# The last stage of a four-layer image kernel, rebuilt on pairs of positions

## The chip, the cores and the metric

The kernel runs on one core of one Trainium2 chip. A time is the device time of one execution in microseconds (us) on that core.

In profile lines PE is TensorE, PEld its weight loads, DVE is VectorE, ACT is ScalarE, POOL is GpSimd, and SPq is the queue of SyncE that issues transfers. "L1168" is a line of the source.

## The reference

Four images of 192 channels and 64x64 points in float32 pass through four layers. The change concerns the third and fourth only. Cut to these:

```python
# layer 3: a depthwise conv whose weights come from the pooled image; of the 3x3 taps only four are kept
pooled = x.mean(axis=(2, 3))
t = relu(gamma * (pooled @ w1.T - running_mean) * rsqrt(running_var + EPS) + beta)
wt = (t @ w2.T + b2).reshape(b * DIM, 1, 3, 3) * MASK        # MASK keeps taps 0, 1, 2 and 3
x = conv(x, wt, groups=b * DIM, padding=1) + bias

# layer 4: sedenion product in windows of 4x4, then an MLP
xn = layer_norm(x, norm1_g, norm1_b)                          # over the 192 channels
xw = get_window(xn)                                           # 16 positions of 192 channels each
xw = xw @ sedenion_full_weight(w_sed)                         # y[k] = sum over s of +-(xw[s] @ w_sed[s ^ k])
y = gelu(reverse_window(xw)) @ proj_w + proj_b
x = x + y
h = gelu(layer_norm(x, norm2_g, norm2_b) @ fc1_w + fc1_b)     # 768 hidden channels
x = x + h @ fc2_w + fc2_b
```

The first two layers are three Mamba blocks. They take the first three quarters of the time and are left as they are.

## The kernel before

192 channels are kept as two chunks of 96 (`CP = 96`). A position of the 4x4 window is a set of 256 columns (`NWIN = 256`, one per window), and `T = 512` columns are two positions. The parts that matter, with cuts marked:

```python
def conv(img):
    ...                                        # pooled sums, squeeze-excite, weights wt of this image
    for s in range(NPOS):                      # 16 positions, 2 chunks, 4 taps: all on DVE
        for k in range(2):
            for tap in (3, 0, 1, 2):
                ...
                nc.vector.scalar_tensor_tensor(o, src, wk, o, ALU.mult, ALU.add)
    return xw

def product(xn, q, background):                # positions 2q and 2q+1
    for h in range(2):
        k = 2 * q + h
        ...
        for m in range(2):                     # output chunk of 96
            for sign, ps in ((1, plus), (-1, minus)):
                of = [s for s in range(NPOS) if signs[s][k] == sign]
                for n, s in enumerate(of):
                    for cc in range(2):        # input chunk of 96
                        nc.tensor.matmul(ps[:, m, :], w["sed"][:, cc, s ^ k, bass.ts(m, CP)],
                                         xn[:, cc, bass.ts(s, NWIN)], ...)
                    if n % 2:
                        background.step()      # post() of the pair before: project, norm, MLP
        nc.scalar.copy(neg, minus)
        nc.vector.tensor_tensor(y[:, :, bass.ts(h, NWIN)], plus, neg, ALU.subtract)

class Norm:                                    # variance as 128x4 numbers, spread again by a matmul
    ...
    nc.tensor.matmul(var[:, q : q + 1], sq[:, k, bass.ts(q, 128)], self.mean_w[:, 0:1], ...)
    nc.scalar.activation(rs, var, AF.Sqrt, bias=self.eps)
    nc.vector.reciprocal(rs, rs)
    ...
    nc.tensor.matmul(rb[:, bass.ts(q, 128)], rs[:, q : q + 1].to_broadcast([128, CP]), self.ident, ...)

for b in range(NB):                            # the serial frame: conv, first norm, product
    xw = conv(img)
    if b + 1 < NB:
        img = load(b + 1)
    for t in range(NT):
        for _ in ln.run(xw[:, :, c], ..., xn[:, :, c]):
            pass
    for q in range(NPOS // 2):
        y = product(xn, q, background)
        background.drain()
        background.add(post(b, q, xw, y, outs))
    background.drain()
```

## Time and profile before

| | before |
|---|---|
| time, median of the runs beside the changed kernel | 13043.12 us (13041.86 to 13043.54) |
| last stage in the profile | 9637 to 13042.5 us |
| opening (stage start to first product matmul) | 131 us |
| one image | 840 us |
| two positions of one image | 85.4 us |

The prediction shows the page's slices, three stretches of the last stage, and the timeline of the product. One line completes them, the opening by stretch: busy us of PE, weight loads, DVE, ACT and POOL (with the number of instructions), then granted clock, DMA share and GB/s.

```profile
9637.00:9768.00 131.00, 14.82 (x52) 10.15 (x53) 80.42 (x140) 4.26 (x7) 1.87 (x8) 0.50 0.36 66
```

In 131 us DVE works 80 and PE 15. What fills DVE are the conv taps, 649 ns each in the mean of 384, with no idle time ahead of them: the conv is bound by DVE alone, four times over.

### The profile page before, as it was taken

What the parts mean: (1) busy time and instruction counts of PE and PEld (TensorE: products, weight loads), DVE (VectorE), ACT (ScalarE), POOL (GpSimd) and SP (SyncE); (2) the same over time, 40 slices, a digit from 0 to 9 for tenths busy, and PEclk for the clock granted to TensorE, in tenths of its full rate; (3) what the DMA queues carried; (4) which work ended last, traced back from release to release, by engine and by line L of the source; (5) the groups of instructions that cost most, each with busy time, mean ns of one, the idle gap of its engine ahead of it and who ended that gap; (6) DMA issues with size and microseconds to landing.
All of it is one profiled execution on the core that took longest, in us unless ns stands there. A gap on an engine that the chain in (4) does not pass through costs nothing.

```text
span 13042.5 us, 102087 instructions
## 1 busy us (share of the span) xinstructions
PE 10585.6 (81%) x34064; PEld 4515.3 (35%) x34064; DVE 9231.5 (71%) x7740; ACT 6226.9 (48%) x8329; POOL 6565.0 (50%) x3394
## 2 busy tenths in 40 slices
PE   6777777777777777758898998989859979889799
PEld 2222222222222222222333333333326646566465
DVE  7999999999999999979887788787831030220300
ACT  5566556566556556646666656665611111111111
POOL 5777777777777777756555555555610000000000
PEclk7777777777777776767888888888869979889899
DMA  5666666666666666645444444444420000000000
GB/s 144 164 166 166 162 167 169 162 165 166 160 166 166 161 168 167 160 131 149 126 130 130 125 129 129 129 130 127 128 40 3 5 12 5 5 13 5 3 5 5
DMA packets 842950, 1449.85 MB, mean 111 GB/s; under 512 B 129194, under 2 KB 162254, under 8 KB 842326
## 3 DMA queue, kind: packets, MB, share of 16 engines
q1 hardware_dynamic: 841662, 1440.15, 42.7%
q8 instruction: 270, 4.42, 0.2%
q10 hardware_dynamic: 760, 3.16, 0.1%
q14 instruction: 258, 2.11, 0.1%
HBM read 1254.25 MB, written 188.74 MB: 111 GB/s over the span
## 4 chain that ended last, share of the span: by engine, by line
PE 44%; DVE 34%; ACT 8%; POOL 6%; issue 5%; DMA 2%; SPq 1%; DVEq 0%; ACTq 0%; POOLq 0%
DVE h L601 21%; DVE h L586 10%; PE plus L1168 7%; PE minus L1168 7%; PE ps_dw L986 5%; POOL h L614 4%; PE ps_in L483 4%; PE ps_o L331 3%; PE ps_conv L501 3%; PE ps_h L408 3%; PE ps_o L417 3%; PE y L623 2%; ACT dA L595 2%; DVE xw L1153 2%; ACT L595 1%
## 5 line engine op out<-in xcount | busy, mean ns | idle before, releaser
L601 DVE TENSOR_TENSOR_SCAN h<-dA,m_state,h 128x512 f32<-128x512 f32 x4608 | 5614.2, 1266 | 423.2 <-ACT dA L595 316.0
L614 POOL TENSOR_TENSOR h<-h,C 128x2048 f32<-128x2048 f32 x1152 | 5213.5, 4526 | 93.3 <-POOL m_state L613 1.0
L595 ACT ACTIVATE dA<-dtE,m_A 128x512 f32<-128x512 f32 x4608 | 3096.2, 687 | 2177.5 <-DVE h L601 2047.6
L586 DVE TENSOR_TENSOR h<-dtxE,B 128x2048 f32<-128x2048 f32 x1152 | 2602.9, 2259 | 109.4 <-DMA dtxE<-r_dtx 109.4
L623 PE MATMUL y<-h,gather 128*32 128x512 f32 x9216 | 1631.9, 789 | 1033.8 <-POOL h L614 1006.2
L613 POOL COPY m_state<-h 128x4 f32<-128x4 f32 x1152 | 215.2, 187 | 1922.4 <-DVE h L601 1888.9
L1179 DVE TENSOR_TENSOR y<-plus,neg 96x512 f32<-96x512 f32 x64 | 44.0, 687 | 1600.8 <-ACT neg L1178 1600.8
L483 PE MATMUL ps_in<-xT,m_in_w 96*128 96x512 f32 x1536 | 992.4, 803 | 73.9 <-ACT z L486 72.5
L1168 PE MATMUL plus<-xn,t 96*96 96x256 f32 x4352 | 1013.4, 380 | 0.0
L501 PE MATMUL ps_conv<-raw,m_conv 128*128 128x512 f32 x2112 | 951.3, 598 | 0.0
L1168 PE MATMUL minus<-xn,t 96*96 96x256 f32 x3840 | 934.3, 396 | 12.6 <-ACT xn L390 12.3
L623 PEld LDWEIGHTS y<-h,gather 128*32 128x32 f32 x9216 | 201.6, 121 | 2137.9 <-POOL h L614 1639.0
L1106 POOL MEMSET img<- 96x132 f32 x4 | 0.8, 204 | 1794.9 <-DVE xw L1153 1794.9
L1168 PEld LDWEIGHTS plus<-xn,t 96*96 96x96 f32 x4352 | 710.0, 163 | 338.0 <-issue 132.8
L1168 PEld LDWEIGHTS minus<-xn,t 96*96 96x96 f32 x3840 | 645.0, 170 | 252.1 <-ACT xn L390 29.1
L483 PEld LDWEIGHTS ps_in<-xT,m_in_w 96*128 96x128 f32 x1536 | 377.0, 260 | 782.0 <-issue 520.5
L986 PE MATMUL ps_dw<-strip,dw 96*96 96x512 f32 x1152 | 640.1, 710 | 0.0
L1178 ACT COPY neg<-minus 96x512 f32<-96x512 f32 x64 | 36.7, 573 | 1165.1 <-PE minus L1168 1165.1
L537 POOL TENSOR_TENSOR raw<-dt,xc 128x1536 f32<-128x1536 f32 x96 | 330.5, 3442 | 504.7 <-ACT dt L536 504.7
L501 PEld LDWEIGHTS ps_conv<-raw,m_conv 128*128 128x128 f32 x2112 | 387.2, 189 | 540.1 <-issue 532.8
L527 PE MATMUL ps_dt<-dbl,m_dt_w 12*128 12x512 f32 x576 | 432.0, 860 | 158.2 <-ACT dbl L519 118.1
L573 PE MATMUL B<-dbl,spread 44*128 44x512 f32 x384 | 341.6, 986 | 237.8 <-DVE h L586 237.8
(142 smaller groups left out, 11488.1 us busy)
## 6 DMA issues: line engine op xcount, KB each, us to landing
dtE<-r_dt SPq DMA_DIRECT2D x2304, 256.0 KB, 4.5
dtxE<-r_dtx SPq DMA_DIRECT2D x2304, 256.0 KB, 6.0
r_dt<-dt SPq DMA_DIRECT2D x96, 768.0 KB, 4.0
r_dtx<-raw SPq DMA_DIRECT2D x96, 768.0 KB, 7.8
x<-x SPq DMA_DIRECT2D x64, 384.0 KB, 3.1
xt<-in_x SPq DMA_DIRECT2D x32, 384.0 KB, 6.7
x<-o SPq DMA_DIRECT2D x32, 384.0 KB, 2.6
img<-x SPq DMA_DIRECT2D x8, 1536.0 KB, 20.8
```

Of the source, the lines that this page charges most:

```text
L331: nc.tensor.matmul(ps, self.w2[:, m, bass.ts(k, CP)], h[:, m, :], start=(m == 0), stop=(m == NH - 1),)
L408: nc.tensor.matmul(ps, self.w1[:, k, bass.ts(m, 128)], x[:, k, :], start=(k == 0), stop=(k == 1))
L483: nc.tensor.matmul(ps, self.in_w[:, k, bass.ts(e, 128)], xn[:, k, :], start=(k == 0), stop=(k == 1))
L501: nc.tensor.matmul(ps, self.conv[:, d, j, :], raw[:, d, j : j + T], start=(j == 0), stop=(j == K - 1))
L527: nc.tensor.matmul(ps, self.dt_w[:, bass.ts(d, 128)], dbl[:RK, :], start=True, stop=True)
L586: self.nc.vector.tensor_tensor(h, u[k // 2][1], u["B", k % 2].unsqueeze(1).broadcast_to([128, 4, T]), ALU.mult,)
L595: self.nc.scalar.activation(dA, u[k // 2][0][:, j, :], AF.Exp, scale=self.A[:, k, j : j + 1])
L601: self.nc.vector.tensor_tensor_scan(h[:, j, :], u.pop(("dA", k, j)), h[:, j, :], self.state[:, k, j : j + 1], ALU.mult, ALU.add,)
L614: nc.gpsimd.tensor_tensor(h, h, u["C", k % 2].unsqueeze(1).broadcast_to([128, 4, T]), ALU.mult)
L623: self.nc.tensor.matmul(u["ys"][32 * j : 32 * j + 32, :], self.ex.gather[:, i // 2, :], h[:, j, :], start=(i == 0), stop=(i == 3),)
L986: nc.tensor.matmul(ps, dw[:, k, j, :], s[:, k, dy : dy + rows, dx : dx + HW], start=(j == 0), stop=(j == 8),)
L1168: nc.tensor.matmul(ps[:, m, :], w["sed"][:, cc, s ^ k, bass.ts(m, CP)], xn[:, cc, bass.ts(s, NWIN)], start=(n == 0 and cc == 0), stop=(n = ...
```

## The change

It has three intents. First, fill the array: two window positions (4 apart, one row of the 4x4 window: `position(g, 0)` and `position(g, 1)`) have 384 channels together, which are three chunks of 128 instead of four of 96. The outer two chunks need all 128 columns; the middle one is half of one position and half of the other, and is made by two 64-column matmuls meant to run side by side. Second, make the next image's conv and first norm while the product of this image runs, through four lanes of generators that get one tick per product step; the normed image waits in DRAM. Third, take mean and variance both by a matrix of ones, so that they come out already spread over 128 partitions. The reciprocal then works on 128x512 instead of 128x4. Besides, one of the four conv taps goes to ACT, the norm's multiply by the reciprocal root goes from DVE to POOL, and the pooled sums come from an accumulated output in the stage before.

```diff
+PIECES = (
+    (0, slice(0, 128), slice(0, 128), 0),
+    (1, slice(0, 64), slice(128, 192), 0),
+    (1, slice(64, 128), slice(0, 64), 1),
+    (2, slice(0, 128), slice(64, 192), 1),
+)
...
+        def each(outs, wt, v, cols):          # middle chunk: 64 rows per position
+            for start in (True, False):
                 for k in range(2):
+                    c, p = (2 * k, ALL) if start else (1, half[k])
+                    nc.tensor.matmul(outs[k], wt[p, c, cols[k]], v[p, c, :], start=start, stop=not start)
+        def normed(v, which):
+            mean = bank("mean")
+            each(full(mean), ones, v, [ALL, ALL])
...
+            nc.scalar.activation(sq, d, AF.Square)
+            yield 5
+            var = bank("var")
+            each(full(var), ones, sq, [ALL, ALL])
...
+            nc.scalar.activation(rs, var[:, :, W], AF.Sqrt, bias=eps)
+            nc.vector.reciprocal(rs, rs)
+            nc.gpsimd.tensor_tensor(d[:, 0::2, :], d[:, 0::2, :], rs, ALU.mult)
...
+            yield 12
...
+        def product(b, k):
+            for m, sides in enumerate((
+                    [(0, ALL, slice(0, 128))],
+                    [(0, half[0], slice(128, 192)), (1, half[1], slice(192, 256))],
+                    [(1, ALL, slice(256, 384))])):
+                made = [terms(k, side) for side, _, _ in sides]
+                for n in range(3 * NP):
+                    for t, (_, parts, cols) in zip(made, sides):
...
+                    lanes.tick()
...
+        def mlp(b, k, x3, xn2):
...
+            nc.scalar.activation(h, h, AF.Gelu)
+            yield 5
...
+        lanes.add(2, prepare(0))
+        lanes.until(lambda: (0, NP - 1) in ready)
         for b in range(NB):
+            if b:
+                lanes.until(lambda: (b, NP - 1) in ready)
+                fetch(b)
+                lanes.until(lambda: (b - 1, NP - 1) in added and not lanes.lanes[0])
             if b + 1 < NB:
+                lanes.add(2, prepare(b + 1))
+            for k in range(NP):
+                if k > 1:
+                    lanes.until(lambda: (b, k - 2) in closed)
+                lanes.add(0, project(b, k, product(b, k)))
+        lanes.drain()
```

A `yield 5` in a lane means: go on five ticks later. One tick is one product step, that is one 256-column matmul slot (two records in the trace, 0.4315 us, as the prediction works out).

## The prediction

> **What bounds the kernel now.** I read the page first, for where the stages lie, then busy time by stretch, the groups of the last stage, and the timeline record by record.
>
> ```profile
> PE 10585.6 (81%) x34064; PEld 4515.3 (35%) x34064; DVE 9231.5 (71%) x7740; ACT 6226.9 (48%) x8329; POOL 6565.0 (50%) x3394
> ...
> PE   6777777777777777758898998989859979889799
> DVE  7999999999999999979887788787831030220300
> PEclk7777777777777776767888888888869979889899
> ```
>
> In slices 1 to 28 DVE carries the two Mamba stages, which the change leaves alone (but for one accumulated output on 64 evictions). From slice 30 on, PE is all there is. The timeline puts the last stage from 9637 us (constants and image asked for) to 13042.5: 3405 us. All of the change is there.
>
> ```profile
> 9900.00:10200.00 300.00, 300.00 (x1177) 193.03 (x1176) 26.53 (x39) 53.35 (x59) 0.00 (x0) 0.98 0.03 6
> 10475.00:10608.00 133.00, 52.52 (x138) 25.87 (x137) 77.79 (x142) 17.37 (x20) 0.75 (x3) 0.62 0.10 18
> 12986.00:13043.00 57.00, 37.72 (x86) 15.85 (x84) 7.11 (x10) 13.93 (x15) 0.00 (x0) 0.81 0.07 14
> ```
>
> Busy us of PE, weight loads, DVE, ACT and POOL, then clock, DMA share, GB/s. Within an image PE is full (300 of 300). Between images 131 to 134 us pass with PE under half busy: 28 us of the last position's remaining work, then 78 us of DVE alone (the conv). An image lasts 840 us (conv starts at 9689, 10530, 11366, 12209). The bound is PE columns in the product, and a serial conv four times.
>
> ```profile
> 10205.26 7.93 PE L1168 MATMUL plus<-xn,t 96*96 96x256 f32 x36
> ...
> 10213.03 6.21 PE L1168 MATMUL minus<-xn,t 96*96 96x256 f32 x28
> ```
>
> 36 records in 7.77 us: 0.2158 us each. An f32 matmul leaves two records (8192 in the two product groups, 4096 matmuls in the code), so 256 columns cost 0.4315 us, whatever rows and columns of the array they fill: 96x96 of 128x128 is 56%. Check: two positions take 128 x 0.4315 = 55.2 us of product plus 28.7 of projection, norm and MLP = 83.9; the trace repeats every 85.4.
>
> **What the Trainium skill says.** "TensorEngine Tiling (Array Packing)", Key Properties: tiles run in parallel, and changing the tiling mode drains the array. The trace agrees on both for column tiles:
>
> ```profile
> 976.56 4.89 PE L501 MATMUL ps_conv<-raw,m_conv 128*128 128x512 f32 x11
> 981.38 1.06 PE L623 MATMUL y<-h,gather 128*32 128x512 f32 x8
> 982.38 1.98 PE L501 MATMUL ps_conv<-raw,m_conv 128*128 128x512 f32 x4
> ```
>
> Eight gather records on four 32-column tiles take 1.06 us with drain: two slots of 0.43, not eight. From full mode to tiles the start-to-start step is 0.522 us against 0.429 inside a mode: 0.093 us a switch. No trace of before shows two row tiles at once; for those I rely on the page.
>
> "VectorE: DVE Perf Modes", First, the fixed hardware budget: Reciprocal is an iterative divide with a repeat count of 8. The trace agrees as far as it goes:
>
> ```profile
> L377 DVE RECIPROCAL ln_rs<-ln_rs x64: 177/178/179, 9763.3 to 13000.9; 128x4 f32<-128x4 f32 x64
> L1093 DVE RECIPROCAL bn_s<-bn_s x1: 155/155/155, 9661.4 to 9661.4; 48x1 f32<-48x1 f32 x1
> ```
>
> Three more elements cost 23 ns, near 8 ns each, where a tensor_tensor element costs about 1.3 (687 ns for 512). The change makes the operand 512 wide.
>
> "TensorE: Matmul & The Clock Gate", What's actually happening: a low-activity window of about 3.4 us halves the clock. The trace agrees: the burst of N=1 variance matmuls is followed by product records at half speed.
>
> ```profile
> 9977.83 1.59 PE L368 MATMUL var<-mean_w,xn 96*128 96x1 f32 x13
> 9979.28 4.02 PE L1168 MATMUL minus<-xn,t 96*96 96x256 f32 x10
> ```
>
> Ten records in 4.0 us instead of 2.3: some 1.7 us lost per burst. The same page (the architectural detail on queue depths) says ACT and DVE are strict FIFO; that decides two terms below.
>
> **The change, part by part.** I counted the built program in its order, with the tiling mode of each matmul, in slots of 0.4315 us.
>
> *PE.* A pair of positions takes 24 full matmuls, 24 pairs on two 64-column tiles, and 24 full: 72 slots instead of 128. Projection: 8 matmuls, 5 slots with pairing. Each norm: mean and variance, each 2 full plus one pair of row tiles: 6 slots. MLP: 18 + 18 slots. Sum 72+5+12+36 = 125 slots = 53.9 us per pair, against 85.4: for 32 pairs 1729 us by my count. There are 1114 changes of mode, x 0.093 = 104 us. Together 1833; 24 of it (image 0's first norm) is in the opening, so 1809.
>
> *Opening.* Image 0's conv and norm are still alone. First half image, shared with 7 MB of weights: about 40 us (39 before). Then DVE goes in strict order: 9 taps x 0.648 = 5.8; wait for mean on a cold PE 2.9; subtractions 1.55; wait for square, variance, root, beyond two taps put in between, 3.1; reciprocal 512 x 8.3 ns + 0.15 = 4.4 (an estimate from the page's count of 8 and DVE's 0.96 GHz): 17.8 us per pair. After four, the second half image must land, some 25 us, because there is one image buffer. 40 + 59 + 25 + 77 + 4 = 205 us, against 131 before.
>
> *Inside a pair.* (a) Second norm's variance waits for subtract and square: 2.8 us against 5 ticks, 0.6. (b) DVE's order is reciprocal, three taps, y, three taps: the next image's mean waits until 4.4 + 3.9 + 0.4 us of DVE work after the root are done, while PE has 14 ticks: 3.3 us. (c) fc2 waits for evacuation, table load 1.28 and Gelu 2.76 against 8 ticks: 1.7. With small waits 5.8 us in 24 pairs; in the last image (b) becomes the MLP's wait for the reciprocal chain, 5 in all for 8: 179 us. A wait of 3 us should, like the N=1 burst now, cost a half-clock window: 32 x 1.7 = 54.
>
> *Between images.* The normed image comes back from DRAM (4.2 MB, 16 to 20 us) only after the last product has read the old one, and the next load queues behind it on SP (3.1 MB, 21 us in the trace), landing some 44 us after the product's end. The conv's first tap on ACT waits for it, and everything behind it on ACT too, MLP evictions included. PE has about 12 us of work: 32 lost, twice. Into image 1 there is no fetch: 10. Into the last there is no load: 17. Together 91.
>
> *End.* After the last product 5.5 + 16 us of PE work lie on a chain of some 55 us (project, norm, reciprocal, MLP, store): 33 idle.
>
> Sum: 205 + 1809 + 179 + 54 + 91 + 33 = 2371 us, 9638 + 2371 = 12009. Gone: three convs and drains of 131 us, 56 slots a pair, the pooled sums (4 x 8.7 us).
>
> **Rivals.** *DVE or ACT becomes the bound.* DVE per pair: y 1.3, x3 1.7, subtractions 3.1, reciprocals 8.8, taps 5.8, evictions 2 = 23 us; ACT about 22. Against some 65 us neither can; only latency counts. *Tiles don't overlap.* If row tiles run one after the other, 384 pairs add 166 us: 12175; if column tiles too, some 410 more: about 12585. The gather speaks against the second. *A cheap reciprocal.* At 0.7 us for 512 elements (b) and most of the MLP's wait go, and 30 us of the opening: about 11840. The slope speaks against it. *The transfers are hidden*: without the boundary terms 11920. *Worse*: bank conflicts, two two-bank buffers among four lanes, add 3 us to each pair: 12105.
>
> **Range and chances.** The PE sum is firm to about 30 us if tiles overlap. Stalls per pair are uncertain by 2 us (64 in all), the opening and the boundaries by 30 to 40 each; row tiles pull up by 166 with one chance in ten, a cheap reciprocal pulls down by 170 with one in ten. 11870 to 12170. Even with both tile rivals the kernel is 3.5% faster, so slower is nearly excluded.
>
> **What would show it.** Product pair matmuls starting within some 10 ns of each other, and so for row tiles; a step of 0.52 at mode changes scaled to 256 columns (about 0.31); reciprocals of 4.4 us, 64 of them; the first product record near 9845; the mean of the first norm and fc2 as PE's largest waits; PE idle 10 to 30 us at three places with ACT's tap waiting for the image; pairs every 63 to 65 us. I am wrong if pairs come at 58 or at 72, if the opening is 130 or 260 us, or if the Mamba stages move by over 20 us.

## The result, and the profile after

The changed kernel takes 12043.35 us (median of four runs, 12039.77 to 12048.52). Ratios here are the mean time of one kernel's fast runs over that of the other's of the same rounds, so not quite the ratio of the medians: 0.9234 (0.9218 to 0.9250). That is 7.7% faster. All outputs are right. Predicted were 12009 us, 11870 to 12170.

The page, same lines as shown of before:

```profile
PE 9661.3 (80%) x32988; PEld 3953.7 (33%) x32988; DVE 9280.3 (77%) x7703; ACT 6324.2 (53%) x8548; POOL 6751.6 (56%) x3584
...
PE   6777777777777777776698899999989859999998
...
DVE  7999999999999999999688888887887442322311
...
PEclk7677777777767767776688888888888869999999
```

PE is busy 924 us less (9661.3 against 10585.6). The dips between the images are gone. One dip in PE and its clock is left, in slice 33, where the opening lies; slices 34 to 40 are nearly full. In the last stage DVE no longer jumps between 0 and 3 tenths but works, after the opening, at 2 or 3 beside PE, and at 1 in the last image, which has none to prepare behind it.

Four stretches of the last stage: the opening, a pair of positions with preparation beside it, a pair of the last image without, and the end. Columns as above.

```profile
10576.30:10647.20 70.90, 64.55 (x337) 43.10 (x336) 21.45 (x27) 20.34 (x27) 5.91 (x6) 0.95 0.02 8
11678.90:11738.80 59.90, 57.64 (x321) 39.49 (x321) 9.94 (x14) 14.58 (x18) 2.69 (x3) 1.00 0.00 1
...
9632.00:9815.00 183.00, 60.08 (x157) 31.11 (x157) 91.96 (x116) 46.72 (x70) 23.46 (x24) 0.50 0.40 81
11981.00:12038.00 57.00, 30.49 (x128) 18.18 (x128) 8.95 (x12) 13.51 (x15) 2.66 (x3) 0.78 0.12 28
```

A pair takes 70.9 us while the next image is prepared and 59.9 otherwise, against 85.4 before. (70.9 is a mean: with preparation beside, the trace has 68 to 74 us from pair to pair, and in the last image 59.9 to 62.3.) The pair without preparation has the full clock (1.00); with it the clock is at 0.95, so some of its matmuls ran at half speed. The opening is longer than before, 183 us against 131.

The timeline of PE during a split third, with the MLP's first layer in between (start, us, engine, line, what, shape, count):

```profile
10604.23 1.52 PE L1219 MATMUL sed_ps<-xn,sed 128*64 128x256 f32 x12
...
10605.67 1.76 PE L1119 MATMUL ps_h<-xn,t_bw 128*128 128x256 f32 x8
...
10607.36 0.65 PE L1219 MATMUL sed_ps<-xn,sed 128*64 128x256 f32 x4
```

Twelve 64-column records pass in 1.44 us up to the next group's start: six record steps of 0.216, not twelve, and what the changes of mode cost. Record by record the two halves start 7 ns apart; so do the 64-row pairs of the norms and of the first MLP layer (`ps_h`).

Two waits of PE stand out. Here is the first norm's mean of the next image, with what happened on the other engines ahead of it. In brackets: idle time just before, and what ended it.

```profile
10590.37 3.35 DVE L1144 RECIPROCAL rs<-rs 128x512 f32<-128x512 f32 x1 [2.94 <-ACT rs L1143]
...
10593.64 3.01 DVE L1172 SCALAR_TENSOR_TENSOR xw<-img,wt,xw 128x256 f32<-128x256 f32 x3
...
10596.68 0.42 DVE L1229 TENSOR_TENSOR y<-sed_ps,neg 128x256 f32<-128x256 f32 x1
...
10597.02 2.07 DVE L1172 SCALAR_TENSOR_TENSOR xw<-img,wt,xw 128x256 f32<-128x256 f32 x3
...
10599.15 1.98 PE L1119 MATMUL mean<-xw,ones 128*128 128x256 f32 x6 [2.72 <-DVE xw L1172]
```

DVE works in order: 3.35 us of reciprocal of the other norm, three taps, y, three taps. PE idles 2.72 us until the last tap. This is the queue that the prediction described.

And here is the second MLP layer, waiting for the Gelu on ACT:

```profile
10621.88 0.69 ACT L1127 ACTIVATE hid<-ps_h,t_bv 128x512 f32<-128x512 f32 x1 [2.45 <-PE ps_h L1119]
10622.47 1.57 ACT L1127 ACTIVATE xo<-d,t_bv 128x256 f32<-128x256 f32 x3
10623.94 0.59 ACT L1127 ACTIVATE xo<-d,turned 128x256 f32<-128x256 f32 x1
...
10624.80 1.28 ACT L1270 ACT_TABLE_LOAD   x1
10626.09 2.76 ACT L1270 ACTIVATE hid<-hid 128x3072 f32<-128x3072 f32 x1
...
10628.91 4.16 PE L1283 MATMUL ps_o<-hid,t_bw 128*128 128x256 f32 x12 [3.27 <-ACT hid L1270]
```

Between the last evacuation (`hid<-ps_h`) and the table load stand four outputs of the next image's first norm (`xo`) and a copy. They hold the Gelu up by 2.3 us of the 3.27 that PE waits. Four such outputs stand there in 18 of the 32 pairs. The twelve records of fc2 behind the wait take 4.16 us where twelve steps at full speed are 2.6: part of them ran at the halved clock.

**Where the stage's 2406 us go.** From the records of PE I took the steps from start to start. A full-speed record steps 0.2158 us, a side-by-side partner under 0.03. What a step has above 0.2158 goes to one of four places: a mode change, the record right after one, a half-clock stretch, or a wait. Start of stage, opening and end are read off directly.

| us | predicted | after |
|---|---|---|
| stage begins | 9638 | 9632.3 |
| opening | 205 | 182.7 |
| matmul slots | 1705 | 1714.8 |
| drain at a change of mode (1008 beside no wait or half clock, of 1079 after the opening; predicted 104 for 1114 in the stage) | 104 | 92.9 |
| the record after a change | none | 84.7 |
| half clock | 54 | 91.5 |
| waits in pairs, boundaries and end | 179 + 91 + 33 = 303 | 229.4 + 9.3 after the last PE record |
| end of profiled run | 12009 | 12038 |

These sums are my own sorting of the trace; where a change of mode falls into a wait or a half-clock stretch, it counts there. The granted clock is a check of one of them: after the opening it stood at 0.5 for 198 us, so that at most 99 us were lost to it. The experiments test the terms.

### The profile page after: what moved, and what is told of

Read it like the earlier page. It is cut to its first block, busy times and chain, and to the rows that moved or that the text cites. A ratio compares the mean times of both kernels' runs of the same rounds, so it can differ in the third digit from the quotient of the medians.

```text
span 12038.0 us, 100646 instructions
## 1 busy us (share of the span) xinstructions
PE 9661.3 (80%) x32988; PEld 3953.7 (33%) x32988; DVE 9280.3 (77%) x7703; ACT 6324.2 (53%) x8548; POOL 6751.6 (56%) x3584
## 5 line engine op out<-in xcount | busy, mean ns | idle before, releaser
L1145 POOL TENSOR_TENSOR d<-d,rs 128x512 f32<-128x512 f32 x64 | 86.2, 1347 | 2162.7 <-DVE rs L1144 2162.7
L1219 PE MATMUL sed_ps<-xn,sed 128*128 128x256 f32 (+1 forms) x6144 | 1120.9, 392 | 0.0
L1219 PEld LDWEIGHTS sed_ps<-xn,sed 128*128 128x128 f32 (+1 forms) x6144 | 779.6, 166 | 301.2 <-issue 152.4
L357 PE MATMUL ps_o<-hid,t 128*96 128x512 f32 x768 | 430.9, 708 | 76.5 <-DVE xn L309 63.5
L1286 DVE SCALAR_TENSOR_TENSOR o<-ps_o,t_bv,x 128x256 f32<-128x256 f32 x96 | 65.3, 680 | 520.1 <-PE ps_o L1283 520.1
L1229 DVE TENSOR_TENSOR y<-sed_ps,neg 128x256 f32<-128x256 f32 x96 | 40.8, 425 | 549.2 <-ACT neg L1228 548.4
L457 PE MATMUL ps_x<-xc,m_pack 128*44 128x512 f32 x576 | 351.7, 760 | 125.3 <-ACT dA L535 75.7
```

What stands on the lines that cost most here:

```text
L357: nc.tensor.matmul(ps, self.w2[:, m, bass.ts(k, CP)], h[:, m, :], start=(m == 0), stop=(m == NH - 1),)
L457: nc.tensor.matmul(ps, self.x_w[:, d, :], xc[:, d, :], start=(d == 0), stop=(d == ND - 1))
L1219: nc.tensor.matmul(ps[parts, int(sign < 0), :], sed[i ^ k][:, c, cols], xn[b, i][:, data, :], start=(n == 0 or t[n - 1][3] != sign), stop= ...
```

## The experiments

All are variants of the changed kernel and were timed in three batches; in each, the kernel before ran alongside (13043.54, 13046.24 and 13044.32 us). Since variants of different batches are compared with the changed kernel's 12043.35 us, differences under some 3 us are not used. In the profiled runs the last stage begins anywhere from 9632 to 9642 us though nothing ahead of it differs, so openings are counted from its start.

My theory was that PE's slots carry the time and that, on top of them, each prepared pair loses about 7 us in waits, most of it in two (fc2 for its Gelu, the mean for DVE's queue), and some 4 us more in the half-clock stretches that such waits cause. The rivals were that a removed wait only reappears at the next dependency, and that the wide reciprocal costs nothing to PE because it lies beside the product.

**fc2 six ticks later.**

```diff
             nc.scalar.activation(h, h, AF.Gelu)
-            yield 5
+            yield 11
```

> Edit: the MLP lane waits 11 ticks instead of 5 between the Gelu of the hidden layer and the first fc2 matmul. Theory (what lies above the slots of PE are single waits and the half-clock windows they cause): the changed kernel waits 87 us in all at fc2, 2 to 3.5 us a pair, and in the pairs with preparation a half-clock window of some 1.8 us follows. Both go: 87 + 24 x 1.8 = 130 us at best, so 11910 to 11960 us. Rival (the wait is only moved: PE is in order, and what comes after fc2 was about to wait as well): 12020 to 12065 us, with the wait in another group.

Measured: 11938.87 us, ratio to before 0.9153 (0.9139 to 0.9166), 104 us under the changed kernel. The group of fc2 in the last stage of the changed kernel, then in this run (busy us, mean ns | idle ahead, and what ended most of it):

```profile
L1283 PE MATMUL ps_o<-hid,t_bw 128*128 128x256 f32 (+1 forms) x1536 | 299.9, 407 | 80.3 <-ACT hid L1270 80.3
```

```profile
L1283 PE MATMUL ps_o<-hid,t_bw 128*128 128x256 f32 (+1 forms) x1536 | 271.1, 385 | 14.9 <-ACT hid L1270 14.9
```

The idle time falls by 65 us, and busy time by 29 as well, since fewer matmuls run at half clock. By the sorting of steps: waits for fc2 -68, half clock -29, the rest -9 together. The wait did not reappear elsewhere. The result is within the expected range: the Gelu was late, and the schedule gave it too few ticks.

**The first norm's mean eight ticks later.**

```diff
         def first_norm(b, g):
 
+            yield 8
             d = yield from normed(xw[b, g], 1)
```

> Edit: the first norm of the next image starts 8 ticks later, so that its mean matmul comes after the conv's taps that queue behind the reciprocal on DVE. Theory: of the 64 us that PE waits at this mean some 45 are in the pairs; they go, with the half-clock window behind each (24 x 1.8 = 43): 11950 to 11985 us. Rival (the norm now falls into the MLP's part and makes it wait, or the window has another cause): 12020 to 12065 us.

Measured: 11941.13 us, ratio 0.9155 (0.9141 to 0.9169), 102 us under the changed kernel, somewhat more than expected. Groups of the mean and of the first MLP layer, in the changed kernel:

```profile
L1119 PE MATMUL mean<-xw,ones 128*128 128x256 f32 (+1 forms) x200 | 61.4, 532 | 68.4 <-DVE xw L1172 68.4
...
L1119 PE MATMUL ps_h<-xn,t_bw 128*128 128x256 f32 (+1 forms) x1536 | 359.6, 433 | 28.7 <-ACT xn L1127 28.7
```

and in this run:

```profile
L1119 PE MATMUL mean<-xw,ones 128*128 128x256 f32 (+1 forms) x200 | 45.3, 425 | 5.2 <-DVE xw L1172 5.2
...
L1119 PE MATMUL ps_h<-xn,t_bw 128*128 128x256 f32 (+1 forms) x1536 | 354.6, 426 | 57.2 <-ACT xn L1127 57.2
```

Here the rival is partly right. The mean's wait goes from 64 to 5 us by my sorting, but fc1's grows from 34 to 67. That the whole still gains 102 comes from two sides: half clock -50, and fc2's wait -27. The traces show what released fc2: in the changed kernel four `xo` outputs stand in the 4.5 us ahead of 18 of the 32 Gelus, in this run ahead of none.

**The reciprocal taken away.** The root and the reciprocal become one activation, so DVE has nothing to do there. Tried before that, and never run: a power on DVE (did not compile), an Rsqrt activation (the library refuses it) and a division on POOL (did not compile).

```diff
-            nc.scalar.activation(rs, var[:, :, W], AF.Sqrt, bias=eps)
-            nc.vector.reciprocal(rs, rs)
+            nc.scalar.activation(rs, var[:, :, W], AF.Abs_reciprocal_sqrt, bias=eps)
```

> Edit: square root on ACT and reciprocal on DVE become one absolute-reciprocal-square-root activation; 64 reciprocals of 3.35 us go from DVE. Theory (the reciprocal on the strict queue of DVE makes the next image's mean wait and lengthens opening, boundaries and end): opening 8 x 3.35 = 27, 24 pairs x (3.0 + 1.8) = 115, last image 8 x 1, boundaries and end 4 x 3.35 = 13: 160 us less, so 11880 us. Rival (DVE is off the path within the product, as its busy share of 30% of a pair suggests; only opening, boundaries and end gain): 40 to 50 us less, so 12000 us.

Measured: 11905.53 us, ratio 0.9130 (0.9116 to 0.9143): 138 us gained. ACT's part stays what it was (64 activations of 687 ns; 69 table loads in the stage before the edit and 71 after it), so what goes is DVE's reciprocal. The part "variance by ones" thus carries a cost of 138 us in it, although DVE is not the busiest engine. Sorted: opening -21, mean -58, fc1 -26, half clock -44, mode changes +9 (there are 1079 in both; fewer are now covered by half clock). The gain was smaller than I expected by some 25 us.

In the trace of the changed kernel all 64 are alike (ns of the shortest, median and longest, and where they lie):

```profile
L1144 DVE RECIPROCAL rs<-rs x64: 3352/3353/3354, 9683.5 to 11994.0; 128x512 f32<-128x512 f32 x64
```

**Reciprocal and fc2 together.** Both edits above (the first and the third).

> Edit: the single activation in place of root and reciprocal, and fc2 6 ticks later. Theory: the two waits are separate, so the gains of the two runs add (138 + 104 = 242 us): 11790 to 11820 us. Rival (they shared half-clock windows or one wait hid the other): 11850 to 11900 us.

Measured: 11798.36 us, ratio 0.9046 (0.9033 to 0.9060), 245 us under the changed kernel; the single gains add to 104 + 138 = 242. So neither wait hid the other. Half clock is down from 91.5 to 14.6 us: nearly all of it was a consequence of these waits.

**The two halves in turn.** The same matmuls, but the 24 of one half and then the 24 of the other, so that neighbours use the same tile and can't lie side by side.

```diff
-                for n in range(3 * NP):
-                    for t, (_, parts, cols) in zip(made, sides):
+                done = 0
+                for t, (_, parts, cols) in zip(made, sides):
+                    for n in range(3 * NP):
                         ...
-                    lanes.tick()
+                        done += 1
+                        if done % len(sides) == 0:
+                            lanes.tick()
```

> Edit: in the middle third of the product the 24 matmuls of the first 64-column tile come one after the other, then the 24 of the second, instead of in pairs; same instructions, no two on different tiles side by side. Theory (a slot of 0.4315 us serves both tiles): 32 x 24 x 0.4315 = 331 us more, less some waits that this fills: 12300 to 12375 us. Rival (weight loads or the waits bound this third, so that pairing is worth little): under 100 us more.

Measured: 12245.29 us, ratio 0.9389 (0.9373 to 0.9404), 202 us over the changed kernel. The same stretch of PE as shown above:

```profile
10668.17 2.80 PE L1220 MATMUL sed_ps<-xn,sed 128*64 128x256 f32 x12
```

Twelve records take 2.80 us instead of 1.52. Slots grow by 318 us (768 lost pairings x 0.4315 would be 331), but waits fall by 72 and half clock by 48: my reading is that the longer product gives every lane more time per tick. I had allowed for it too little: the result lies under the expected 12300, though far from the rival's "under 100". Pairing on column tiles is real, and in this schedule worth 202 us.

**The preparation alone.** The second intent undone: each image's conv and first norm run before its product, and no trip through DRAM.

```diff
         for b in range(NB):
             if b:
-                lanes.until(lambda: (b, NP - 1) in ready)
-                fetch(b)
                 lanes.until(lambda: (b - 1, NP - 1) in added and not lanes.lanes[0])
-            if b + 1 < NB:
-                lanes.add(2, prepare(b + 1))
+            lanes.add(2, prepare(b))
+            lanes.until(lambda: (b, NP - 1) in ready)
```

> Edit: the preparation of each image (load, conv, first norm) stands alone before its product, as in the kernel before; nothing goes ahead to DRAM; product, norm and MLP stay as changed. Theory: the 24 pairs with preparation come down from some 71 us to the 60 of the last image (-264 us), and three times an opening like the first one is added: from the first one, 183 us, less the wait for constants, with the last pair's MLP beside the start: 150 to 180 each, 450 to 540. Net 190 to 280 us more: 12235 to 12320 us. Rival (preparation beside the product is free, so that undoing it adds the whole openings): 12490 us or more. Rival (it is worth nothing): 12045.

Measured: 12235.75 us, ratio 0.9380 (0.9365 to 0.9396), 192 us over the changed kernel. By stretch, one opening between products and one pair:

```profile
10277.80:10456.40 178.60, 82.42 (x258) 41.81 (x256) 98.02 (x115) 59.63 (x84) 26.13 (x27) 0.61 0.21 36
10610.30:10670.20 59.90, 57.64 (x321) 39.47 (x321) 9.94 (x14) 14.58 (x18) 2.69 (x3) 1.00 0.00 1
```

Every pair now takes about 59.9 us, but three stretches of 177 to 182 us stand between the products. From the first product matmul of an image to that of the next are 632, 631 and 636 us here, and 553, 563 and 566 in the changed kernel: 216 more in all. The last image's product takes 30 less (453 against 483), and 186 of the 192 us are found. The result is at the lower edge of what was expected (12235).

**Padded instead of row tiles.** The middle chunk's 64-row matmuls of mean, variance and fc1 become full ones with zeros in half the weights: no pairing of rows, and no change of mode for them. `neg` went to one buffer to make room.

```diff
-            each(full(mean), ones, v, [ALL, ALL])
+            each_full(full(mean), ones, ones_half, v, ALL)      # likewise var and fc1
```

> Edit: in both norms and in fc1 the two 64-row matmuls of the middle chunk become two 128-row matmuls on weights filled up with zeros: no row tiles there; 320 slots more (138 us), 430 changes of mode fewer. Theory: at 0.18 us a change of mode the 430 give back 76 us, so 60 us slower, 50 to 75: 12090 to 12120 us. Rival A (only the drain of 0.09 counts, as in the prediction): 98 us slower, 12140 us. Rival B (row tiles gain nothing once their changes are paid): 12030 to 12060 us.

Measured: 12121.7 us, ratio 0.9293 (0.9279 to 0.9307), 78 us over the changed kernel. Slots +127, drain -33, the record after a change -36, opening +7, other terms +11. So 362 changes fewer (those beside no wait or half clock, of 398 after the opening) were worth 69 us, or 0.19 us for each, twice the 0.093 of the drain alone. The result lies 2 us above the expected range and 18 under rival A, so the run speaks for the term that the prediction lacked, while its size comes from my sorting. The single `neg` buffer is no rival: no wait for it shows in this run's trace. The rival that row tiles gain nothing (12030 to 12060) falls.

**Reciprocal, fc2 and the order of the thirds.** The split third comes first, which by my count leaves fewer changes of mode.

```diff
-            for m, sides in enumerate(
-                (
-                    [(0, ALL, slice(0, 128))],
-                    [(0, half[0], slice(128, 192)), (1, half[1], slice(192, 256))],
-                    [(1, ALL, slice(256, 384))],
-                )
+            for m, sides in (
+                (1, [(0, half[0], slice(128, 192)), (1, half[1], slice(192, 256))]),
+                (0, [(0, ALL, slice(0, 128))]),
+                (2, [(1, ALL, slice(256, 384))]),
             ):
```

> Edit: as the run before, and the third on 64-column tiles comes first in each product instead of in the middle, where fewer matmuls of other modes fall between its pairs: 972 changes of mode in the program instead of 1096. Theory: a change of mode costs some 0.18 us (0.09 to drain, 0.04 to 0.10 for a weight load that can't run ahead), so 124 fewer are 22 us: 11770 to 11795 us. Rival (waits at other places decide): within 10 us of the run before, either way, or slower.

Measured: 11782.26 us, ratio 0.9032 (0.9019 to 0.9046), 16 us under the run with reciprocal and fc2 (the batch is the same). Counted in the trace, the changes after the opening fell from 1061 to 937, the 124 expected. By my sorting, in which 159 fewer stand beside no wait or half clock, that brought 15 us of drain and 7 of the record behind it; half clock took 9 back.

**The mean too.** The edit of the mean's eight ticks added to the last one.

> Edit: the version with the single activation, the later fc2 and the split third first, and on top the first norm 8 ticks later. Theory: inside the pairs its mean no longer waits, so nothing is gained there; in the opening DVE now works at the next pair's taps while PE makes the mean (some 2.6 us idle a pair): 15 to 30 us less, 11750 to 11770 us. Rival (the later norm collides with the MLP's parts, or DVE's wait moves to ACT's tap): 11775 to 11830 us.

Measured: 11744.46 us, ratio 0.9005 (0.8990 to 0.9020), 38 us less again: waits -22, opening -9, half clock -6. That is more than expected, and from another place: the theory saw the gain in the opening, but most of the 22 us are fc2's wait (21 us to 5), since the `xo` outputs ahead of the Gelu are gone here too. It is much less than the 102 us which the same edit brought alone: the mean itself waited only 6 us before this edit, against 64, the reciprocal having gone from the queue.

**All later.** And the variance seven ticks after the mean instead of five.

```diff
             nc.scalar.activation(sq, d, AF.Square)
-            yield 5
+            yield 7
```

> Edit: as the run before, and the variance of every norm 7 ticks after its mean instead of 5. Theory: PE waits some 25 us in all for the squares, 0.4 to 0.6 us a pair; that goes: 10 to 25 us less than the run before. Rival (the second norm's chain gets longer and fc1 waits instead): within 10 us of the run before, either way.

Measured: 11739.75 us, ratio 0.8999 (0.8986 to 0.9013). The 5 us gained lie in the rival's range, but not for its reason: most of the variance's waits went (23 to 11 us) and fc1's did not grow, but the opening got 5 us longer. This is the fastest kernel, 2.5% under the changed one and 10% under before. Here is its stretch of 1185 us, and the same stretch of the changed kernel:

```profile
9815.00:11000.00 1185.00, 1170.79 (x6546) 822.15 (x6544) 287.40 (x497) 402.36 (x536) 112.88 (x127) 1.00 0.16 36
```

```profile
9815.00:11000.00 1185.00, 1073.90 (x5613) 719.95 (x5612) 369.03 (x462) 347.61 (x463) 104.41 (x113) 0.95 0.14 33
```

PE is busy 1171 of 1185 us at full clock. What is left in it is 1713 us of slots, 164 of mode changes and their records, and 60 of waits and half clock.

One by one the runs undo the column pairs of the product (202 us), the preparation beside the product (192) and the row pairs of norms and fc1 (78). No run undoes the step from chunks of 96 to chunks of 128, which by count of slots (128 to 96 in a product, before any pairing) is worth 32 x 32 x 0.4315 = 442 us, nor the matrix of ones or the pooled sums by themselves. That these make up most of the rest of the 1000 us rests on the counts, with 0.2158 us a record in both traces.

## Why the prediction was right

The sign, the mechanism of the gain (slots saved by filling the array, and the preparation beside the product) and the time held (12043 against 12009, inside the range), but that the total came so close is luck: errors cancel in it. One of the prediction's own signs failed. It wanted pairs every 63 to 65 us and called itself wrong at 72; its terms give 64.7 for a prepared pair, and 70.9 were measured. That is some 150 us too little for 24 pairs (about 65 of it the record after a change, 48 half clock, 34 waits), made good by some 78 too much for the boundaries between images and 22 for the opening.

**Slots.** Right. 1715 us against 1705, since both kinds of tiles lie side by side. In a prepared pair slots take 54.1 us, predicted 53.9. (32 x 125 slots are 1726 us, not the 1729 of the text; the 1705 fit 1726 less the 20.7 us of image 0's first norms.)

**Changes of mode.** The price of 0.093 us was right and carried over (a step of 0.309 instead of 0.216). It was taken for the whole price of a change, and that step failed. The record after the change steps 0.320 us for 128 columns and 0.260 for 64: another 0.104 or 0.045 us, 85 us in all. My reading is that its weight load can't be hidden behind a running matmul when the array has just been drained. The trace fits: inside a mode the load for a record starts one record ahead (at 10605.777 for the record of 10605.991), at a change the load starts with its own record (10605.669 and 10605.671). The padded run confirms the size, and no run isolates the mechanism. The term could have been read before the change: behind the gather in the prediction's own lines, the step from 982.375 to 982.908 is 0.533 us where 0.429 is usual, the same 0.104.

**Half clock.** Right in kind, mis-sized in number. A wait of 2.7 to 3.3 us does cost a half-clock stretch, but a prepared pair has two such waits, so it loses 3.7 us and not 1.7; the last image's pairs have no wait of that length (the longest are 1.5 to 2 us), and their clock stays full (1.00). Predicted 32 x 1.7 = 54, measured 91.5.

**Waits in a pair.** For the mean: predicted 3.3 us, measured 3.0, by two errors that cancel. The reciprocal is 3.35 us, not 4.4. The taps are slower, as the group shows:

```profile
L1172 DVE SCALAR_TENSOR_TENSOR xw<-img,wt,xw 128x256 f32<-128x256 f32 x288 | 222.4, 780 | 88.6 <-ACT xw L1127 68.0 <-issue 14.4
```

780 ns in the mean against the 648 assumed: 178 taps that lie beside no multiply of POOL take 675 ns, the 110 that do take 949. The Trainium skill, "SBUF — State Buffer", section "Who interferes with whom", says that a DVE instruction with two SBUF inputs contends with a GpSimd instruction that reads SBUF. The trace agrees: taps have two inputs, and the multiply by `rs` moved to POOL with this change. For fc2: predicted 1.7 us, about what the last image's pairs have, but 3.4 in the 18 pairs in which `xo` outputs stand ahead of the Gelu. The step that failed counted only evacuation, table load and Gelu, and not the first norm's outputs that stand in the same ACT queue. Prepared pairs wait 7.2 us, not 5.8.

**The opening.** 183 us, not 205. The pace of a pair was right (18.3 us from reciprocal to reciprocal, predicted 17.8), but again by errors that cancel: nine taps take 7.3 us, not 5.8, and the reciprocal 3.35, not 4.4. What failed are the two transfers. The first tap of DVE ran 31 us after the stage began, not 40, and the second half image cost 4.4 us, not 25. On DVE's timeline the reciprocals on the two sides of it are 22.7 us apart (9720.07 and 9742.78), the others 18.3.

**Boundaries between images.** Predicted 10 + 32 + 32 + 17 us lost; this is the largest error besides the prepared pairs. The eight intervals from image 0 to image 1 (Gelu of y to Gelu of y) add up to 567 us, eight times 70.9, so nothing is lost there beyond what preparation costs. (The interval across the boundary is 80.5 us, but the one before it, with nothing left to prepare, is 59.9.) Into the last image the interval is 72.9 us against 59.9, so 13 us where 17 were predicted. The issue times show why:

```profile
10344.43 11.46 SPq L1194 DMA_DIRECT2D xn<-ahead  x6
...
10355.99 0.37 SPq L1050 DMA_DIRECT2D img<-x  x1
...
10376.23 0.83 ACT L1127 ACTIVATE xw<-img,t_bv,wt 128x256 f32<-128x256 f32 x1
```

The prediction let the fetch begin when the product ends. In fact all eight tiles were asked for while the product's last matmuls ran (until 10355.5), two of them from 10336.74 on and the six of the line from 10344.43 on: each tile comes free as soon as the last third has read its last term. The image load followed at once, and the conv's first tap ran 21 us after the product, not 44. PE filled those 21 us with what was left of the last pairs and, from 10368 us, with the next product, with waits of 1.7 to 3.4 us in between. In the changed kernel only 13 us lie between the last product matmul of an image and the first of the next.

**The reciprocal as a rival.** I gave "a cheap reciprocal" one chance in ten and 11840 us. It was neither cheap (3.35 us) nor 4.4. Taking it away altogether gave 11906.

Altogether: exposed weight loads +85, half clock +37, slots +10; waits, boundaries and end -65, opening -22, drain -11, start -5; net +29 on the profiled run.

## What to carry to other kernels

When two small tiles are put side by side, count every change of tile mode at twice its drain, here 0.19 us against the 0.43 of a slot: it pays if the slots saved are worth more than the changes made. The row tiles here save 320 slots for 430 changes, and giving them up still cost 78 us. When work is interleaved by a fixed number of steps, read each wait's queue on the engine that releases it, including what other lanes put in that queue; here six ticks in one place and eight in another brought 100 us each, where the whole change brought 1000. And look for what a wait causes behind it: of the 245 us that came with the reciprocal and fc2's wait gone, 77 were time at half clock.

## What the Trainium skill lacked or had wrong

- "VectorE: DVE Perf Modes" gives the reciprocal a repeat count of 8 and no time for an element. The prediction took the 8 for cycles. From 4 to 512 elements the duration goes from 178 to 3353 ns, which is 6.25 ns per element; at the page's 0.96 GHz that is six cycles.
- "TensorEngine Tiling (Array Packing)", Key Properties, says that a change of mode drains the array, without a size. The runs show 0.093 us for the drain and a further 0.104 us (128 columns) or 0.045 us (64 columns) at the next record, which no page that I read mentions.
- "TensorE: Matmul & The Clock Gate" puts neighbouring tiles' starts about 4 ns apart; here they are 7 ns apart. It asks for an idle window of about 3.4 us before the clock is halved; here waits of 2.7 to 3.3 us were followed by stretches at half speed.
- "SBUF — State Buffer" says that the loser of the shared port fully blocks, and gives no size for an instruction with two SBUF inputs. The runs show taps of 949 ns beside a POOL multiply and 675 ns elsewhere, so on average 0.27 us lost per tap.
